# A pair loop rewritten as a software pipeline with a fixed issue order on three engines

## The chip, the cores and the metric

One core of a Trainium2 chip. The time is the device time of one execution in microseconds (us). All kernels named here gave the right result. Each measured kernel was run four times or more, beside runs of the kernel before on the same chip. All comparisons use runs in the fast state. A ratio below is the mean time of one kernel's fast runs over the mean of the other's fast runs of the same rounds, so it is not quite the ratio of the medians quoted beside it. The profile's engines are PE (TensorE), PEld (its weight load), DVE (VectorE), ACT (ScalarE), POOL (GpSimd).

## The reference, cut to what matters

```python
# layer 0: every node i against every node j of 3327 (padded to 26 blocks of 128), 64 features
h = relu(layernorm(x))
adj_att = sigmoid(left[:, None] + right[None, :] + b_att[0]) * adj
x_local = logmap(h[:, None, :], h[None, :, :], c)        # a scalar function of i.j times two vectors
support_t = einsum('ij,ijd->id', adj_att, x_local)
x = x + proj(expmap(h, support_t, c), c)                 # the "post step", per node
# layer 1: weights 2^-(k - pos) from a running count of each row's edges
rank = cumsum(adj != 0, axis=1)                          # [...]
x = x + (mask * where(pos > 0, 0.5 ** (k - pos), 0)) @ (relu(layernorm(x)) @ weight) + bias
```

Layer 0 and the running count of layer 1 go through the adjacency matrix together, so that it is read once.

## The kernel before

The columns are cut into four strips of 8, 8, 6 and 4 blocks. In a strip the kernel goes through the rows from the last block to the first, one block of 128 rows per round (two in strip 3, whose rows of the tile are half as long). The order on each engine is left to the scheduler. `T`, `V`, `A` are TensorE, VectorE, ScalarE.

```python
STRIPS = [(0, 8), (8, 8), (16, 6), (22, 4)]
for b0, nb in STRIPS:
    # [...] loads of the strip's iu, iz
    for b in range(nb):                                    # the row `left`, laid over all partitions
        T.transpose(pl[:, b * P : (b + 1) * P], left[:, b0 + b : b0 + b + 1].to_broadcast([P, P]), ident)
    A.copy(left_b[:, :F], pl[:, :F])
    for f0, f1 in hv:                                      # a constant under the count
        T.matmul(pc[:, f0:f1], row1, rowc[:, : f1 - f0], start=True, stop=True, skip_group_check=True)
    for hi in range(NB, 0, -per):                          # one round
        # [...] ad: the adjacency tile by DMA
        V.tensor_scalar(mask[:, :span], ad[:, :span], 0.0, None, op0=ALU.not_equal)        # "mask"
        for j in js:
            # [...] per half: two matmuls into pc, with ca on the last mask and cb on this one ("count")
            if j % (2 if b0 == 0 else 4):
                A.activation(kept, pc[:, :F], AF.Relu)                                      # "the read"
            else:
                V.tensor_scalar(kept, pc[:, :F], 0.0, None, op0=ALU.max)                    # the same on VectorE
        for j in js:
            A.activation(part(sg, j), left_b[:, :F], AF.Tanh, bias=right[:, j : j + 1], scale=0.5)
        V.scalar_tensor_tensor(sg[:, :span], sg[:, :span], 1.0, ad[:, :span], op0=ALU.add, op1=ALU.mult)
        # [...] products of iu and iz with ju and jz into pq
        A.activation(s[:, :span], pq[:, :span], AF.Gelu, scale=-WG / QS)
        A.activation(s[:, :span], s[:, :span], AF.Gelu, scale=WH)
        V.scalar_tensor_tensor(s[:, :span], s[:, :span], WD, sg[:, :span], op0=ALU.add, op1=ALU.mult)
        for j in js:
            # [...] per half: T.matmul(po, hw, s)                                           # "total"
            next(steps, None)                              # one part of the last strip's post step
    # [...] po to SBUF, transposes, two ScalarE copies, the next post step is made ready
```

A post step is some 60 operations on VectorE with three Square and one tanh on ScalarE between them; among them are three reciprocal roots, each of 12 tiny operations of 128x8, nearly every one of which needs the last.

## Time and profile before

The time is 461.0 us (459.1 to 463.9, four runs). The stages below are read from the starts of VectorE's last multiply of a round (`s`): a strip goes from its first `s` to its last, a seam from there to the next strip's first.

| stage before | us |
|---|---|
| start to first `s` | 52.5 |
| strip 0, 1, 2, 3 | 87.0, 92.1, 73.3, 47.7 |
| the three seams | 12.5, 10.45, 9.7 |
| last `s` to the end | 73.9 |

Of the page's list of groups (line, operation, tiles, count, then busy us, mean ns, then us of idle time just before them and what ended it), these two matter later, and of the table of stretches strip 3 (the columns after the stretch are its length, busy us of PE, PEld, DVE, ACT, POOL with counts, the granted TensorE clock, DMA share and GB/s):

```profile
L852 DVE SCALAR_TENSOR_TENSOR s<-s,sg 128x1024 f32<-128x1024 f32 (+1 forms) x91 | 104.8, 1152 | 3.7 <-ACT s L851 3.6
L855 PE MATMUL po<-s,hw 128*65 128x512 f32 (+1 forms) x364 | 165.3, 576 | 11.5 <-DVE s L852 11.1
```
```profile
337.00:385.00 48.00, 40.44 (x126) 13.23 (x125) 46.88 (x98) 46.23 (x68) 1.00 (x1) 0.99 0.34 99
```

VectorE waits 3.7 us for the Gelus in the whole kernel, TensorE 11.5 us for `s`. In strip 3 VectorE is busy 46.9 of 48 us. There is almost nothing to win inside a strip, and less in the seams than their 32.6 us suggest: VectorE is busy in 28.1 of them, with masks, multiplies, reads and the copy of `po`. From the first `s` to the last it stands idle for 12.2 of 332.8 us.

### The profile page before, as it was taken

How to read it: one execution, taken by the hardware profiler on the slowest of the kernel's cores; microseconds unless marked ns; L12 is line 12 of the kernel's file. 1: busy time of each engine (PE TensorE's matmuls, PEld its weight loads, DVE VectorE, ACT ScalarE, POOL GpSimd, SP SyncE). 2: the span in 40 equal slices, each digit the busy share in tenths (PEclk: the TensorE clock that was granted, in tenths of full speed). 3: DMA queues.
4: the chain of work that ended last, by engine and by line, in shares of the span. 5: the costliest groups of instructions: out<-in, count | busy, mean ns of one | idle time of the engine just before them, and what ended most of it. 6: DMA issues, size and time to landing. Idle time of an engine off the chain costs nothing.

```text
span 459.1 us, 4660 instructions
## 1 busy us (share of the span) xinstructions
PE 378.4 (82%) x1484; PEld 153.4 (33%) x1484; DVE 407.1 (89%) x774; ACT 369.2 (80%) x423; POOL 13.3 (3%) x30
## 2 busy tenths in 40 slices
PE   0266699999989799999997999889778897699293
PEld 0035233333323233333333444434322332244152
DVE  3895689999988999999998999999999998999821
ACT  1445989999894999999995999999599995888310
POOL 6000000000000000001000000020000000000000
PEclk9997699999999999999999999999999998899877
DMA  7103354545541444444442444344533420000003
GB/s 201 62 1 72 105 168 143 141 151 163 167 135 46 133 143 140 137 137 137 137 127 75 136 137 140 106 128 125 168 93 111 121 89 1 1 1 1 0 0 82
DMA packets 22840, 47.77 MB, mean 104 GB/s; under 512 B 8652, under 2 KB 9082, under 8 KB 22808
## 3 DMA queue, kind: packets, MB, share of 16 engines
q1 hardware_dynamic: 20522, 46.47, 34.7%
q10 hardware_dynamic: 2062, 0.87, 0.9%
q0 software_dynamic: 224, 0.07, 0.3%
q8 instruction: 13, 0.21, 0.2%
q14 instruction: 19, 0.16, 0.1%
HBM read 45.22 MB, written 0.85 MB: 100 GB/s over the span
## 4 chain that ended last, share of the span: by engine, by line

## 5 line engine op out<-in xcount | busy, mean ns | idle before, releaser
L855 PE MATMUL po<-s,hw 128*65 128x512 f32 (+1 forms) x364 | 165.3, 576 | 11.5 <-DVE s L852 11.1
L842 DVE SCALAR_TENSOR_TENSOR sg<-sg,ad 128x1024 f32<-128x1024 f32 (+1 forms) x91 | 103.5, 1141 | 7.5 <-ACT sg L841 7.3
L852 DVE SCALAR_TENSOR_TENSOR s<-s,sg 128x1024 f32<-128x1024 f32 (+1 forms) x91 | 104.8, 1152 | 3.7 <-ACT s L851 3.6
L841 ACT ACTIVATE sg<-left_b,right 128x1024 f32<-128x1024 f32 (+2 forms) x104 | 102.7, 1001 | 0.1
L851 ACT ACTIVATE s<-s 128x1024 f32<-128x1024 f32 (+1 forms) x91 | 91.4, 1006 | 0.1
L850 ACT ACTIVATE s<-pq 128x1024 f32<-128x1024 f32 (+1 forms) x91 | 87.7, 969 | 2.6 <-PE pq L848 2.6
L829 PE MATMUL pc<-mask,ca 128*128 128x512 bf16 (+1 forms) x175 | 65.7, 375 | 17.3 <-DVE behind_hi L836 7.2
L855 PEld LDWEIGHTS po<-s,hw 128*65 128x65 f32 x364 | 45.2, 138 | 98.9 <-issue 52.7
L847 PE MATMUL pq<-iu,ju 71*128 71x512 f16 (+1 forms) x182 | 67.8, 374 | 11.6 <-ACT s L850 11.6
L830 PE MATMUL pc<-mask,cb 128*128 128x512 bf16 (+1 forms) x182 | 66.7, 376 | 5.3 <-DVE mask L824 5.1
L848 PE MATMUL pq<-iz,jz 128*128 128x512 f16 (+1 forms) x182 | 66.6, 371 | 0.0
L824 DVE TENSOR_SCALAR mask<-ad 128x1024 bf16<-128x1024 f32 (+1 forms) x91 | 59.3, 654 | 3.4 <-PE pc L829 1.8
L894 PE MATMUL pw<-wt,s 128*128 128x512 bf16 (+1 forms) x182 | 41.0, 390 | 12.9 <-DVE s L782 9.2
L834 ACT ACTIVATE behind_hi<-pc 128x1024 uint8<-128x1024 f32 (+2 forms) x37 | 31.8, 860 | 24.3 <-PE pc L830 24.1
L830 PEld LDWEIGHTS <-cb 128*128 128x128 bf16 x182 | 17.9, 99 | 57.8 <-issue 46.6
L834 ACT ACTIVATE behind_lo<-pc 128x1024 uint8<-128x1024 f32 (+2 forms) x33 | 28.2, 853 | 7.1 <-PE pc L830 6.4
L894 PEld LDWEIGHTS <-s 128*128 128x128 f16 x182 | 18.7, 103 | 35.0 <-DVE s L782 9.6
L848 PEld LDWEIGHTS <-jz 128*128 128x128 f16 x182 | 18.1, 99 | 31.5 <-issue 15.3
L829 PEld LDWEIGHTS <-ca 128*128 128x128 bf16 x175 | 17.5, 100 | 30.8 <-issue 19.5
L847 PEld LDWEIGHTS <-ju 71*128 71x128 f16 x182 | 18.1, 100 | 21.4 <-issue 4.8
L836 DVE TENSOR_SCALAR behind_lo<-pc 128x1024 uint8<-128x1024 f32 (+2 forms) x19 | 19.9, 1050 | 1.1 <-PE pc L830 1.1
L771 POOL TENSOR_TENSOR x_sb<-x_sb,bias_b 128x512 f32<-128x512 f32 (+2 forms) x4 | 6.3, 1577 | 418.4 <-DVE w L769 418.4
(209 smaller groups left out, 290.0 us busy)
## 6 DMA issues: line engine op xcount, KB each, us to landing
ad<-in_adj_t SPq DMA_DIRECT2D x65, 512.0 KB, 3.7
ad<-in_adj_t SPq DMA_DIRECT2D x26, 384.0 KB, 3.3
out<-o SPq DMA_DIRECT2D x6, 128.0 KB, 2.0
x_sb<-in_x SPq DMA_DIRECT2D x1, 416.0 KB
x_sb<-in_x ACTq DMA_DIRECT2D x1, 416.0 KB, 6.9
iz<-jz ACTq DMA_DIRECT2D x2, 128.0 KB
iz<-jz SPq DMA_DIRECT2D x2, 128.0 KB, 2.4
iz<-jz SPq DMA_DIRECT2D x2, 96.0 KB
```

The costliest lines, as they stand in the source:

```text
L829: T.matmul(pc[:, f0:f1], ca, before[:, f0:f1], start=False, stop=True, skip_group_check=True)
L830: T.matmul(pc[:, f0:f1], cb, now[:, f0:f1], start=False, stop=True, skip_group_check=True)
L834: A.activation(kept, pc[:, :F], AF.Relu)
L841: A.activation(part(sg, j), left_b[:, :F], AF.Tanh, bias=right[:, j : j + 1], scale=0.5)
L842: V.scalar_tensor_tensor(sg[:, :span], sg[:, :span], 1.0, ad[:, :span], op0=ALU.add, op1=ALU.mult)
L847: T.matmul(part(pq, j, f0, f1), ju[:KB, j, :], iuf[:, f0:f1], start=True, stop=False)
L848: T.matmul(part(pq, j, f0, f1), jz[:, j, :], izf[:, f0:f1], start=False, stop=True)
L850: A.activation(s[:, :span], pq[:, :span], AF.Gelu, scale=-WG / QS)
L851: A.activation(s[:, :span], s[:, :span], AF.Gelu, scale=WH)
L852: V.scalar_tensor_tensor(s[:, :span], s[:, :span], WD, sg[:, :span], op0=ALU.add, op1=ALU.mult)
L855: T.matmul(po[: D + 1, f0:f1], hw[:, j, :], part(s, j, f0, f1), start=j == NB - 1, stop=j == 0)
L894: T.matmul(pw[n], s2[:, j].rearrange("p c d -> p (c d)"), wt[:, f0:f1].bitcast(BF16), start=j == 0, stop=j == NB - 1)
```

## The change

Its intent is to keep the engines running across the seams, by writing the four strips as one list of rounds, and to fix what each engine issues in which order. In round n TensorE totals n-1, multiplies for n+1 and counts for n+2. A strip's `left` row comes by a broadcast DMA from a DRAM copy, and not by transposes. The diff, cut to its core:

```diff
+ON_ACT = ((1, 2), (3, 4), (3, 4), (3, 4))          # share of the reads on ScalarE: nearly as before, 73 reads for 70
-    for f0, f1 in hv:
-        T.matmul(pc[:, f0:f1], row1, rowc[:, : f1 - f0], start=True, stop=True, skip_group_check=True)
+        # [...] strip_in(k), strips 1 to 3:
+            nc.sync.dma_start(S.left[:, : S.F], bass.AP(tensor=left_d.tensor, offset=left_d.offset + S.i0,
+                                                         ap=[[0, P], [1, S.F]]))
+    tc_order = tc.manual_schedule(engines={mybir.EngineType.DVE, mybir.EngineType.Activation, mybir.EngineType.PE})
+    with tc_order:
+        products(0)
+        sigmoids(0)
+        for n in range(R):
+            # [...] m = n + 2; `new` is a strip's first round, `second` its second (strips 1 to 3)
+            if second:
+                steps = strip_out2(k - 1)                # transposes, ScalarE copies, post step
+            elif n:
+                total(n - 1)
+            A.activation(s[:, :w], pq[:, :w], AF.Gelu, scale=-WG / QS)
+            A.activation(s[:, :w], s[:, :w], AF.Gelu, scale=WH)
+            sg_inst[n] = V.scalar_tensor_tensor(sg[:, :w], sg[:, :w], 1.0, ad_of.pop(n)[:, :w], [...])
+            if new:
+                strip_out(k - 1)                         # po to SBUF
+            read()                                       # a VectorE read, if one is due
+            if m < R:
+                edges(m)                                 # mask
+            if two:
+                count(m, js(m)[0])                       # with its ScalarE read, if one is due
+            if n + 1 < R:
+                products(n + 1)
+                sigmoids(n + 1)                          # tanh
+            for _ in js(n):
+                next(steps, None)                        # one part of the post step, as a block
+            # [...] a strip's last round runs the rest of the steps
+            read()
+            if m < R:
+                count(m, js(m)[-1])                      # with its ScalarE read, if one is due
+            V.scalar_tensor_tensor(s[:, :w], s[:, :w], WD, sg[:, :w], op0=ALU.add, op1=ALU.mult)
+            if second:
+                total(n - 1)
```

So on ScalarE a round is: Gelu, Gelu, tanh, and a read of the count of round n+2, which stands ahead of the Gelus of round n+1.

Not shown in the cut, but part of the change: five buffers for `ad` instead of four and two for `left_b` instead of one, the copy of `po` in a buffer of `sg` and its transposes in one of `po` (before: `s` and `pq`), and the range check of the inputs, spread over the first rounds and finished in layer 1.

## The prediction

> **What bounds the kernel now.** The kernel does layer-0 attention over all pairs in four strips of columns (8, 8, 6 and 4 blocks of 128). Each round of a strip makes, per 128x1024 tile: a mask (VectorE), a running count into the PSUM tile `pc` (TensorE) which is then read to bytes (ScalarE or VectorE, "the read"), a tanh, a product `pq` (TensorE), two Gelus (ScalarE), two VectorE multiplies (first `sg`, last `s`), and the total into `po` (TensorE). A strip's result is finished by a post step of some 60 small VectorE instructions that runs during the next strip. Layer 1 follows, from 392 us on. I read the page first (busy shares), then the table of stretches with the cuts at the first and last `s` of each strip, then the timelines of VectorE and ScalarE for start-to-start distances, then the built instruction orders of both kernels.
>
> ```profile
> PE 378.4 (82%) x1484; PEld 153.4 (33%) x1484; DVE 407.1 (89%) x774; ACT 369.2 (80%) x423; POOL 13.3 (3%) x30
> ```
> VectorE is the busiest. The stretches show where:
>
> ```profile
> 52.00:139.00 87.00, 84.10 (x275) 30.05 (x274) 82.35 (x83) 82.07 (x86) 0.00 (x0) 0.97 0.52 154
> 139.00:152.00 13.00, 11.41 (x52) 4.78 (x51) 11.10 (x22) 6.95 (x10) 0.00 (x0) 1.00 0.04 10
> 152.00:244.00 92.00, 85.94 (x283) 29.89 (x283) 90.94 (x152) 90.64 (x98) 2.19 (x1) 1.00 0.49 142
> 244.00:254.00 10.00, 8.33 (x45) 4.07 (x44) 7.95 (x14) 5.38 (x9) 0.00 (x0) 1.00 0.08 29
> 254.00:328.00 74.00, 66.46 (x283) 29.75 (x282) 73.60 (x157) 71.45 (x98) 2.40 (x1) 1.00 0.49 138
> ```
> After the length come PE, weight load, VectorE, ScalarE. In strips 1 and 2 VectorE is busy 91 of 92 and 74 of 74 us; in strip 0 all three engines are above 94%. The seams (139 to 152, 244 to 254, also 328 to 337) lose time.
>
> The prices, from start to start on VectorE in strip 0:
>
> ```profile
> 84.32 0.69 DVE L824 TENSOR_SCALAR mask<-ad 128x1024 bf16<-128x1024 f32 x1
> 84.92 1.22 DVE L842 SCALAR_TENSOR_TENSOR sg<-sg,ad 128x1024 f32<-128x1024 f32 x1
> 86.06 0.69 DVE L824 TENSOR_SCALAR mask<-ad 128x1024 bf16<-128x1024 f32 x1
> 86.66 1.22 DVE L852 SCALAR_TENSOR_TENSOR s<-s,sg 128x1024 f32<-128x1024 f32 x1
> 87.80 1.22 DVE L836 TENSOR_SCALAR behind_hi<-pc 128x1024 uint8<-128x1024 f32 x1
> ```
> A mask costs 0.60, each multiply and a VectorE read 1.135. Strip 0 reads every second count on VectorE: 0.60 + 2.5 x 1.135 = 3.44 us a round. Its `s` tiles run from 52.46 to 139.44, 25 intervals of 3.48: VectorE's issue rate. Strip 1 has a quarter of the reads: 25 x 3.15 = 78.9, plus the post step, 16 tiles of 512 columns at 0.60 and some 47 tiny ones at 0.08: 13.4. Sum 92.3; measured (151.90 to 244.03) 92.1. Strip 2 (254.48 to 327.77) took 73.3 against 60.8 + 13.4. So inside the strips VectorE has no slack, and only the seams can be won.
>
> A tiny operation costs only 0.08 because the scheduler puts it ahead of a big one:
>
> ```profile
> 225.73 0.16 DVE L511 TENSOR_TENSOR rs_t<-rs_t,rs_g 128x8 f32<-128x8 f32 x1
> 225.81 0.69 DVE L824 TENSOR_SCALAR mask<-ad 128x1024 bf16<-128x1024 f32 x1
> 226.41 0.16 DVE L512 SCALAR_TENSOR_TENSOR rn<-rs_t,rn 128x8 f32<-128x8 f32 x1
> 226.49 1.22 DVE L852 SCALAR_TENSOR_TENSOR s<-s,sg 128x1024 f32<-128x1024 f32 x1
> ```
> One after the other, each needing the last, they stand 0.20 apart, as in layer 1:
>
> ```profile
> 433.35 0.17 DVE L507 TENSOR_SCALAR rn<-rs_t 128x4 int32<-128x4 int32 x1
> 433.56 0.16 DVE L510 TENSOR_TENSOR rs_t<-rn 128x4 f32<-128x4 f32 x1
> 433.75 0.16 DVE L511 TENSOR_TENSOR rs_t<-rs_t,rs_g 128x4 f32<-128x4 f32 x1
> ```
> And the hops between engines:
>
> ```profile
> 127.45 1.06 ACT L851 ACTIVATE s<-s 128x1024 f32<-128x1024 f32 x1
> ...
> 128.55 1.23 DVE L852 SCALAR_TENSOR_TENSOR s<-s,sg 128x1024 f32<-128x1024 f32 x1 [0.64 <-ACT s L851]
> ...
> 137.29 1.03 ACT L850 ACTIVATE s<-pq 128x1024 f32<-128x1024 f32 x1
> ...
> 138.35 1.06 ACT L851 ACTIVATE s<-s 128x1024 f32<-128x1024 f32 x1
> ...
> 151.90 1.21 DVE L852 SCALAR_TENSOR_TENSOR s<-s,sg 128x1024 f32<-128x1024 f32 x1
> ...
> 153.27 1.88 PE L855 MATMUL po<-s,hw 128*65 128x512 f32 x4
> ```
> ScalarE to VectorE 0.04; the second Gelu starts 1.06 after the first when nothing stands between; VectorE to the total's first matmul 0.10 to 0.16. A total is 4 matmul passes of 0.43 (1.71), products and count 4 of 0.215 each (0.86). On ScalarE, start to start, tanh costs 1.04, a read 0.90.
>
> **What the skill says.** "Perfetto Trace Analysis", Sequencer Loop: an engine's instructions go into a queue and wait there for their semaphores; so in a fixed order a late operand holds up all behind it. The trace agrees: VectorE stood 0.64 us before `s` above. The same page, Identifying Performance Opportunities, says to improve the most-contended engine by its occupancy, here VectorE. "VectorE: DVE Perf Modes", The DRAIN you can't avoid, measures that a semaphore between chained copies "costs nothing extra". This trace differs for tiny tiles: 0.20 with a dependence, 0.08 without. The measurement decides. "ScalarE: Activation LUTs", What ACT_TABLE_LOAD costs, gives about 280 ns + 0.833 ns per element with a pointer bias, 186 without, and 93 of overlap; for 1024 columns 1.13 and 1.04, here 1.165 (tanh) and 1.03 (Gelu).
>
> **The change part by part.** 1. Removed: the constant matmuls into `pc`, and for strips 1 to 3 the transposes of `left` and their ScalarE copy (1.01 us each, replaced by a DMA issued about three rounds ahead, hidden). All lie at seams.
>
> 2. Fixed order. Per round n: TensorE total(n-1), products(n+1), count(n+2); ScalarE Gelu, Gelu (n), tanh(n+1), read(n+2); VectorE sg(n), read, mask(n+2), one post step, s(n). No big tile's work changes, so VectorE's floor of 3.44 stays. But the order closes a loop: s(n-1) ends; 0.10 to total(n-1), 1.71; products 0.86; count 3 x 0.215 + 0.38 = 1.03; 0.05; read(n+2) on ScalarE 0.90; only then Gelu, Gelu (n+1) 1.06 + 1.07; 0.04; s(n+1) 1.22. Sum 8.04 for two rounds, 4.02 each, wherever the read falls to ScalarE: every second round of strip 0, and rounds two apart in the others. Strip 0: 25 x (4.02 - 3.48) = +13.5.
>
> 3. Post steps in one block per round. The built order shows each reciprocal root as 12 chained tiny operations with nothing between: about 2.3 us instead of 1.0, three times, and the step of 14 behind the tanh 2.5 instead of 1.1. Adding up the steps with 0.20 for a dependent and 0.08 for a free one gives 22.7 instead of 13.4. Strip 1: VectorE alone 78.9 + 22.7 = 101.6, +9.5; taking the loop in the 21 light rounds (84.4) and 2.87 + 2.6 in the four heavy ones (21.9), 106.3, +14. I take +13. Strip 2: the loop at 768 columns is about 3.14 a round; 21 x 3.14 + 19.3 = 85, against VectorE alone 83.5; I take +11. Strip 3 takes two steps a round: 12 x 3.17 + 20.4 (six-block steps) = 58.4 against 47.7 (337.51 to 385.24); some may lie in waits, +10.
>
> 4. Seams. Before, from last `s` to first `s`: 12.5, 10.4, 9.7, sum 32.6. After, the next strip's rounds are already running: VectorE waits for total(n-1) (about 2.2), copies `po` (1.13), mask and s, about 5.5, and the round behind it (transposes, two ScalarE copies) about 1.2 longer: 19 in all. Gain -13.5.
>
> 5. The end: total, copy, transposes straight behind the last `s`, 4.9 instead of 6.7: -1.5 with rounding. The range check's few tiny operations move into layer 1: +1.
>
> Sum: 13.5 + 13 + 11 + 10 - 13.5 - 1.5 + 1 = +33.5; 460.6 + 33.5 = 494.
>
> **The rivals.** (a) The pipeline works as meant: engines even out, tiny operations hide, only the seams change: 460.6 - 15 = 446. For it: the seams' idle time is real. Against it: VectorE is in order, and the chained tiny operations stand in one block. (b) Only VectorE counts, the loop has slack I don't see (the hops are from few instances): 0 + 9.5 + 10 + 10 - 13.5 - 0.5 = +15.5, 476. (c) Loop and heavy rounds add up fully, and the seams give less because the second total of a strip is delayed behind the transposes: about 505. (d) TensorE's clock: slices 4 and 5 of the page show 7 and 6 tenths granted; a loop through TensorE feels that more than a kernel bound by VectorE: +3 to +5.
>
> **Range and chances.** Between (b) and (c), with a little below (b): 472 to 508. Rival (a) is all that gives a gain, and I give it 0.07; a balance within 2% 0.08; slower 0.85.
>
> **What would show it.** Right: in strip 0 the `s` tiles start about 4.0 apart by pairs, ScalarE idles about 1 us before each read, released by the count's matmul, and VectorE waits on ScalarE before `s`; in strips 1 and 2 the rounds with a reciprocal root take over 5 us and VectorE's busy share falls; seams shrink to 5 to 7 us. Wrong: strip 0 still at 3.5 a round (loop not there), or tiny operations 0.08 apart in a block, or seams as long as before. If the reads stop being waited for, the time falls toward 476.

## More of the kernel before

`pc` and `po` have one buffer each in PSUM (two banks each), `pq` has two.

## The result, and the profile after

The changed kernel took 513.24 us (512.39 to 516.8, four runs), the kernel before 461.03 in the same rounds: 1.114 times as long (95% interval 1.106 to 1.122). The direction was as predicted; the size was not, and 513 lies above the range. All outputs are right.

```profile
PE 385.7 (75%) x1442; PEld 153.0 (30%) x1460; DVE 418.8 (81%) x772; ACT 381.7 (74%) x423; POOL 10.6 (2%) x28
```
```profile
L906 PE MATMUL po<-s,hw 128*65 128x512 f32 (+1 forms) x364 | 172.2, 597 | 66.0 <-DVE s L982 65.8
L982 DVE SCALAR_TENSOR_TENSOR s<-s,sg 128x1024 f32<-128x1024 f32 (+1 forms) x91 | 106.0, 1165 | 29.4 <-ACT s L959 29.3
...
L875 ACT ACTIVATE behind_lo<-pc 128x1024 uint8<-128x1024 f32 (+2 forms) x36 | 30.3, 841 | 32.0 <-PE pc L868 31.8
L875 ACT ACTIVATE behind_hi<-pc 128x1024 uint8<-128x1024 f32 (+2 forms) x37 | 31.3, 845 | 26.5 <-PE pc L868 25.6
```

No engine works much longer than before (VectorE 418.8 for 407.1 us), and every share fell. The groups say who waits for whom, and it is a ring: TensorE's total waits 66.0 us for `s` (11.5 before), `s` 29.4 us for the second Gelu (3.7 before), and ScalarE's reads 58.5 us for the count (before, 31.4 us). The stretches of the four strips after:

```profile
51.00:154.00 103.00, 92.92 (x292) 31.57 (x298) 87.93 (x94) 88.89 (x89) 0.00 (x0) 0.97 0.44 129
...
158.00:269.00 111.00, 90.53 (x304) 31.80 (x308) 101.20 (x165) 96.92 (x102) 1.27 (x1) 1.00 0.39 114
273.00:363.00 90.00, 70.80 (x305) 31.38 (x306) 83.03 (x164) 76.41 (x102) 1.27 (x1) 1.00 0.40 114
368.00:443.00 75.00, 55.73 (x143) 18.24 (x144) 56.21 (x125) 49.98 (x72) 1.00 (x1) 0.82 0.18 55
```

In strip 0 VectorE was busy 82 of 87 us, now 88 of 103; in strip 3, 47 of 48, now 56 of 75, with a granted clock of 0.82 instead of 0.99. Set against each other stage by stage (profiled executions of 459.1 and 515.1 us):

| stage | before | after | difference | predicted |
|---|---|---|---|---|
| strip 0 | 87.0 | 102.6 | +15.6 | +13.5 |
| strip 1 | 92.1 | 110.1 | +18.0 | +13 |
| strip 2 | 73.3 | 89.7 | +16.4 | +11 |
| strip 3 | 47.7 | 74.6 | +26.9 | +10 |
| three seams | 32.6 | 14.9 | -17.7 | -13.5 |
| start, end of the loop, layer 1 | 126.4 | 123.3 | -3.1 | -0.5 |

The differences add up to +56.1, the spans differ by 56.0. Two cautions: the profiled execution of the change was the slowest of its four (516.8 us, the others 512.4 to 514.0), so some 3 or 4 us may be that execution's own; and a stage can gain by handing work to its neighbour. VectorE was busy in 12.0 of the 14.9 us of the seams after, for 28.1 of 32.6 before, so most of the seams' -17.7 is work that now lies in the strips.

The loop itself, as the timeline shows it in strip 0 (start and duration in us; in brackets the idle time before, and what ended it):

```profile
61.94 1.02 ACT L875 ACTIVATE behind_hi<-pc 128x1024 uint8<-128x1024 f32 x1 [1.25 <-PE pc L868]
...
65.00 1.22 DVE L982 SCALAR_TENSOR_TENSOR s<-s,sg 128x1024 f32<-128x1024 f32 x1 [1.23 <-ACT s L959]
...
66.14 1.22 DVE L961 SCALAR_TENSOR_TENSOR sg<-sg,ad 128x1024 f32<-128x1024 f32 x1
...
66.28 1.93 PE L906 MATMUL po<-s,hw 128*65 128x512 f32 x4 [0.80 <-DVE s L982]
...
67.28 1.22 DVE L882 TENSOR_SCALAR behind_hi<-pc 128x1024 uint8<-128x1024 f32 x1
...
68.41 0.68 DVE L856 TENSOR_SCALAR mask<-ad 128x1024 bf16<-128x1024 f32 x1
...
69.15 0.81 PE L868 MATMUL pc<-mask,cb 128*128 128x512 bf16 x2
...
69.99 1.02 ACT L875 ACTIVATE behind_hi<-pc 128x1024 uint8<-128x1024 f32 x1 [0.95 <-PE pc L868]
```

From one ScalarE read to the next but one round's is 69.99 - 61.94 = 8.05 us; the working of the prediction had 8.04. It splits into 3.06 us from the read through the two Gelus to `s`, and 4.99 us from `s` back to the read. The prediction followed that second part through TensorE: total at 66.28, then products and count, 69.15. But VectorE closes it at the same length: behind `s` come `sg`, its own read and the mask, and the mask ends at 69.09, just before the count that needs it starts at 69.15. From here on nobody can say from the trace alone which of the two holds the loop.

The post steps in strip 1, in the same view:

```profile
212.03 1.23 DVE L982 SCALAR_TENSOR_TENSOR s<-s,sg 128x1024 f32<-128x1024 f32 x1 [0.80 <-ACT s L959]
...
215.91 0.17 DVE L508 TENSOR_TENSOR rs_t<-rn 128x8 f32<-128x8 f32 x1
216.12 0.17 DVE L509 TENSOR_TENSOR rs_t<-rs_t,rs_g 128x8 f32<-128x8 f32 x1
...
217.26 1.22 DVE L982 SCALAR_TENSOR_TENSOR s<-s,sg 128x1024 f32<-128x1024 f32 x1
```

The tiny operations stand 0.20 apart, and this round took 217.26 - 212.03 = 5.23 us. The four heavy rounds of strip 1 (three with a reciprocal root, one with the 14 operations behind the tanh) took 5.54, 5.48, 5.23 and 5.17, together 21.4 where 21.9 was predicted; the other 21 took (110.05 - 21.42) / 21 = 4.22 instead of 4.02. Among these are two of 5.07 and 5.63 us, in which a VectorE read and a part of the post step fall together.

For strip 3, the view of waits on VectorE (what waited, for whom, then us in all, times, longest), and below it TensorE's costliest wait there:

```profile
DVE sg L961 <- ACT sg L889: 7.5, 5, 2.7
DVE t L782 <- ACT dt L779: 2.3, 1, 2.3
DVE t L765 <- ACT dt L762: 2.3, 1, 2.3
DVE u L732 <- ACT dt L725: 2.0, 1, 2.0
```
```profile
PE po L906 <- DVE s L982: 15.9, 7, 3.8
```

With a tanh of the post step (1.6 us) these are 15.7 us of VectorE standing still, against 1.1 us idle in all before. The prediction has no term for either kind.

### The profile page after: what moved, and what is told of

It reads as the page before. It is cut to its first block, busy times and chain, and to the rows that moved or that the text cites. A ratio compares the mean times of both kernels' runs of the same rounds, so it can differ in the third digit from the quotient of the medians.

```text
span 515.1 us, 4572 instructions
## 1 busy us (share of the span) xinstructions
PE 385.7 (75%) x1442; PEld 153.0 (30%) x1460; DVE 418.8 (81%) x772; ACT 381.7 (74%) x423; POOL 10.6 (2%) x28
## 4 chain that ended last, share of the span: by engine, by line
## 5 line engine op out<-in xcount | busy, mean ns | idle before, releaser
L906 PE MATMUL po<-s,hw 128*65 128x512 f32 (+1 forms) x364 | 172.2, 597 | 66.0 <-DVE s L982 65.8
L982 DVE SCALAR_TENSOR_TENSOR s<-s,sg 128x1024 f32<-128x1024 f32 (+1 forms) x91 | 106.0, 1165 | 29.4 <-ACT s L959 29.3
L889 ACT ACTIVATE sg<-left_b,right 128x1024 f32<-128x1024 f32 (+2 forms) x104 | 100.0, 974 | 0.0
L868 PE MATMUL pc<-mask,cb 128*128 128x512 bf16 (+1 forms) x178 | 65.2, 376 | 21.2 <-DVE mask L856 20.5
L896 PE MATMUL pq<-iu,ju 71*128 71x512 f16 (+1 forms) x182 | 70.0, 384 | 0.0
L897 PE MATMUL pq<-iz,jz 128*128 128x512 f16 (+1 forms) x182 | 68.2, 382 | 0.0
L867 PE MATMUL pc<-mask,ca 128*128 128x512 bf16 (+1 forms) x165 | 61.5, 373 | 4.6 <-ACT behind_hi L875 2.3
L875 ACT ACTIVATE behind_lo<-pc 128x1024 uint8<-128x1024 f32 (+2 forms) x36 | 30.3, 841 | 32.0 <-PE pc L868 31.8
L896 PEld LDWEIGHTS <-ju 71*128 71x128 f16 x182 | 18.5, 102 | 34.3 <-issue 21.9
L1002 ACT ACTIVATE wt<-behind_lo 128x3328 uint16<-128x3328 uint8 x6 | 17.4, 2963 | 0.0
L882 DVE TENSOR_SCALAR behind_lo<-pc 128x1024 uint8<-128x1024 f32 (+2 forms) x16 | 17.1, 1067 | 0.0
```

What stands on the lines that cost most here:

```text
L867: T.matmul(S.pc[:, f0:f1], ca, S.before[:, f0:f1], start=False, stop=True, skip_group_check=True)
L868: T.matmul(S.pc[:, f0:f1], cb, now[:, f0:f1], start=S.first, stop=True, skip_group_check=True)
L875: A.activation(kept, S.pc[:, : S.F], AF.Relu)
L889: A.activation(part(n, sg, j), S.left[:, : S.F], AF.Tanh, bias=right[:, j : j + 1], scale=0.5)
L896: T.matmul(part(n, pq, j, f0, f1), ju[:KB, j, :], S.iu[:, f0:f1], start=True, stop=False)
L897: T.matmul(part(n, pq, j, f0, f1), jz[:, j, :], S.iz[:, f0:f1], start=False, stop=True)
```

## The experiments

Theory at the start: the loop through ScalarE's read costs strip 0 and the light rounds, blocks of chained tiny operations cost the heavy rounds, and in strip 3 the read in the middle of a round holds up the tanhs. Rivals: the loop is held by VectorE's order or by the one `pc` buffer and not by TensorE; and removing any one wait brings out another. The strip lengths in this table (us, first to last `s`) come from each run's profile; medians and ratios to the kernel before from all fast runs.

| kernel | median | ratio (95%) | strip 0 | strip 1 | strip 2 | strip 3 |
|---|---|---|---|---|---|---|
| before | 461.0 | 1 | 87.0 | 92.1 | 73.3 | 47.7 |
| after | 513.2 | 1.114 (1.106, 1.122) | 102.6 | 110.1 | 89.7 | 74.6 |
| late_read | 502.5 | 1.093 (1.088, 1.097) | 92.4 | 105.1 | 89.6 | 74.9 |
| spread | 497.6 | 1.082 (1.078, 1.086) | 102.6 | 107.3 | 86.2 | 62.1 |
| mid_read | 513.8 | 1.119 (1.114, 1.124) | 101.6 | 110.5 | 91.2 | 69.3 |
| lag2 | 507.5 | 1.101 (1.096, 1.106) | 101.3 | 108.4 | 89.4 | 67.4 |
| mask_first | 516.7 | 1.123 (1.118, 1.127) | 104.4 | 110.3 | 90.4 | 72.8 |
| mask_lag2 | 512.7 | 1.115 (1.109, 1.121) | 103.4 | 110.1 | 89.0 | 68.5 |
| all3 | 477.7 | 1.036 (1.031, 1.040) | 92.1 | 102.7 | 83.4 | 59.2 |
| all3_lag2 | 474.8 | 1.029 (1.025, 1.033) | 88.7 | 102.4 | 83.2 | 56.9 |
| before_row | 449.7 | 0.974 (0.971, 0.978) | 87.5 | 89.1 | 73.8 | 42.9 |
| auto | 444.8 | 0.967 (0.963, 0.970) | 87.7 | 95.2 | 77.3 | 44.6 |
| only_act | 496.1 | 1.076 (1.071, 1.082) | 101.4 | 107.0 | 90.2 | 60.6 |
| only_dve | 478.5 | 1.038 (1.031, 1.044) | 89.5 | 100.2 | 82.7 | 66.6 |
| only_pe | 459.6 | 0.998 (0.996, 1.001) | 95.5 | 97.1 | 79.1 | 47.5 |

The medians of the kernel before in the four groups of rounds lay between 460.3 and 461.1, so medians of different groups may be set side by side.

### The read behind the Gelus (late_read), or between them (between_read)

```diff
-            A.activation(kept, S.pc[:, : S.F], AF.Relu)
+            act_reads.append((kept, S.pc[:, : S.F]))
             A.activation(s[:, :w], pq[:, :w], AF.Gelu, scale=-WG / QS)
+            # between_read: act_read() here
             A.activation(s[:, :w], s[:, :w], AF.Gelu, scale=WH)
+            # late_read: act_read() here
```

> The ScalarE read that ends a round is emitted behind the two Gelus of the next round instead of ahead of them; nothing else changes. Theory (the loop of 8.04 us per two rounds goes through that read, and the post steps add on top of it): without it strip 0 falls from 4.10 to about 3.5 us a round (102.6 to 89 us from first to last s tile), strip 1 from 110 to about 102 (VectorE with its block of chained tiny operations, worked out as 101.6), strip 2 from 89.7 to about 84, strip 3 stays near 72 to 75; the time 513 to about 484. Rival (only the post step's chained operations and the clock cost time, the read merely waits where there is slack): strip 0 stays at 4.0, the time within 2% of 513.

> The same read emitted between the first and the second Gelu of the next round. Theory: the loop loses one Gelu of 1.06 us, 6.98 instead of 8.04 per two rounds, so 3.49 a round, just above VectorE's 3.44; strip 0 about 88 us, the time within 1% of the kernel with the read behind both Gelus. Rival (it is not the length of the loop that matters but that ScalarE waits for the count at all): a gain of about half or less.

late_read took 502.5 us where 484 was expected. Strip 0 fell from 102.6 to 92.4, with steady rounds of 3.63 instead of 4.03, and strip 1 from 110.1 to 105.1. The read no longer waits; it starts as soon as ScalarE is free:

```profile
69.10 1.01 ACT L884 ACTIVATE behind_hi<-pc 128x1024 uint8<-128x1024 f32 x1
```

Strips 2 and 3 did not move; 84 us had been expected for strip 2, and why it stayed is open. between_read took 494.7 us, 1.073 times before (1.067 to 1.078), from three fast runs; its profiled run was slow, so its strips are not used. It had been expected within 1% of late_read and is 1.5% faster; why is not shown. Moving the read won back 11 to 18 of the 52 us. Strip 0 did not come all the way to 3.5: in late_read VectorE now waits a little for the tanh, which has the read ahead of it.

### Post steps handed out in small pieces (spread)

```diff
-        rsqrt(pool, rn, t0, nb)                      # 12 tiny operations in a block
+        yield from rsqrt_g(pool, rn, t0, nb)         # a yield after each dependent one
         A.activation(dt, u, AF.Square)
-        yield
+        yield HOLD                                   # two slots free before its result is used
```

A slot is behind `sg`, behind a VectorE read, ahead of `s` and behind `s`.

> The post step cut into single dependent operations, one in each gap between wide VectorE instructions, with two gaps left free behind each result that comes from ScalarE; the reads stay as in the change. Theory: strip 0 unchanged at 102 us; strip 1 falls from 110 to the loop's 4.02 x 25 = 100.5 to 102, strip 2 from 89.7 to about 80; strip 3 loses the 8.2 us in which VectorE waits for ScalarE inside the post step and the block stalls, 74.6 to about 60; the time 513 to about 481. Rival (the loop through the read is all, the tiny operations sit in its slack): strips 1 and 2 within 2 us of before, the time 505 or more.

497.6 us: 15.6 us better than the change, of which strip 3 alone gave 12.5 in the profiles (74.6 to 62.1). In strips 1 and 2 the gain was 2.8 and 3.5 us, less than half of what was expected. In strip 1 the heavy rounds exceed the others by 21.4 - 4 x 4.22 = 4.5 us in all, so no more than that was to be had while the loop held the others; I had not done this sum, and this half of the expectation missed. In strip 3 the 8.2 us of waits for the Squares and the post step's tanh are gone from the trace, `sg` still waits 5.0 us for the tanh, and the clock is 0.97; how much the smaller pieces and how much the free slots did, one run cannot tell.

### The middle read of strip 3 behind the tanhs (mid_read)

```diff
             if two:
-                count(m, js(m)[0])                   # its ScalarE read at once, ahead of both tanhs
+                count(m, js(m)[0])
             sigmoids(n + 1)
+            if two:
+                act_read()
```

> Only in strip 3 (two blocks a round): the ScalarE read in the middle of a round is emitted behind the two tanh instead of ahead of them. Theory: the tanh no longer waits for count, which waits for the total, which waits for s; the 7.5 us in which VectorE waits in strip 3 for the tanh before sg go away; strip 3 from 74.6 to 67 or 68, the time 513 to about 506, strips 0 to 2 unchanged. Rival (strip 3 is slow because of TensorE's clock of 0.82 and the post step's waits): strip 3 within 2 us of 74.6.

In the profile strip 3 fell by 5.3 us, a little less than expected, but the median did not move (513.8 for 513.2). The profiled run of the change was the slowest of its four (516.8), that of mid_read the fastest of its own (511.5), so part of the 5.3 us may be the choice of runs. This one is inconclusive in time. Its trace is clearer: in strip 3 `sg` no longer waits for the tanh at all (7.5 us before), so the read's place made that wait; but the first Square of the post step is now waited for 5.1 us instead of 2.0, which takes part of the gain back.

### What closes the loop (lag2, mask_first, mask_lag2)

```diff
-                total(n - 1)                         # lag2, mask_lag2: one round later
+                total(n - 2)
-            read()                                   # mask_first, mask_lag2: VectorE's read after the mask
             edges(m)
+            read()
```

> The total into po lags by two rounds instead of one (total(n-2) in round n; at a seam both are done at once); the reads stay ahead of the Gelus as in the change. Theory: the loop is broken at another of its links, since count and read no longer stand behind a total that waits for the newest s; strip 0 falls from 4.10 to 3.5 or 3.6 a round as with the late read (the read's place was never the fault by itself), strips 1 and 2 as with the late read (about 105 and 88 us), the time about 500. Rival (the place of the read on ScalarE is what costs, whatever stands behind it): strip 0 stays at 4.0 a round, the time within 1% of 513.

> VectorE's mask for the round after next is emitted ahead of its read instead of behind it; total one round late and ScalarE's read ahead of the Gelus as in the change. Theory after the two-rounds-late total left strip 0 at 4.05: there are two loops of the same length, both through ScalarE's read and the two Gelus; one comes back over s, total, products and count (8.04), the other over s, sg, VectorE's read and mask to count (about 8.1). This run breaks only the second: strip 0 stays at 4.0 to 4.1 a round, the time within 1% of 513. Rival (the mask loop alone binds): strip 0 at 3.6 or less.

> Mask ahead of the read, and the total two rounds late. Theory of the two loops: now both are broken though ScalarE's read still stands ahead of the Gelus; the second loop is shorter by one VectorE instruction of 1.135, 6.98; strip 0 at 3.5 to 3.65 a round, 88 to 92 us; the time about 490 to 497. Rival (the read's place on ScalarE costs in itself): strip 0 at 4.0, the time above 503.

If TensorE's total held the loop, lag2 would cut strip 0. It stayed at 4.05 us a round, as its rival said. The count now waited for the mask:

```profile
107.45 0.38 PE L868 MATMUL pc<-mask,cb 128*128 128x512 bf16 x1 [0.22 <-DVE mask L856]
```

If the mask were the only other way, mask_lag2 would have brought 3.5. It brought 8.27 for two rounds and 512.7 us, so its rival was right; mask_first gave the same 8.27, near the 4.0 to 4.1 a round that its theory said. The reason is in the trace of mask_lag2: VectorE's read of the single `pc` buffer now ends later, and the next count starts only behind it:

```profile
99.81 0.38 PE L867 MATMUL pc<-mask,ca 128*128 128x512 bf16 x1 [1.20 <-DVE behind_lo L882]
```

So between `s` and the next ScalarE read lie three ways back, through the total, the mask and the VectorE read, the last two over the same engine, and all about 5 us long (4.99 us in the change, 5.00 in lag2, 5.26 in mask_lag2). Of the cuts that were tried only the one in the part that they share, the read ahead of the Gelus, paid in strip 0: late_read. lag2's gain of 5.8 us in the median lies in strip 3 (-7.2 in the profiles), not in the loop.

### The mended pipeline (all3, all3_lag2)

all3 is late_read with spread and the middle read behind the tanhs; all3_lag2 adds lag2.

> Late read, single post operations in the gaps and strip 3's middle read behind the tanh together. Theory (the causes are separate and share the strips): strip 0 3.70 as with the late read alone, strip 1 about 97, strip 2 about 79, strip 3 about 55; the time about 513 - 10 - 13 - 11 - 20 = 459, within 1% of the kernel before. Rival (they hide behind one another or a further wait takes their place): 475 or more.

> The same with the total two rounds late as well. Theory: TensorE then never waits for the newest s, so strip 0 comes to VectorE's 3.44 to 3.5 a round, strip 1 to 93 to 95, strip 2 to 75 to 77, strip 3 to 50 to 52; the time about 450, below the kernel before thanks to the shorter seams. Rival (the fixed order keeps some 0.2 us of wait in each round): about as long as without the lag.

They took 477.7 and 474.8 us and remain 3 to 4% slower than the kernel before; the rivals' numbers held, not the theory's. all3_lag2's strip 0 is nearly mended (88.7 against 87.0), strips 1 to 3 are not (102.4, 83.2 and 56.9 against 92.1, 73.3 and 47.7). In strip 1, VectorE's `sg` waited in 8 times for the tanh, which now stands behind the read, 4.6 us in all3 and 4.3 in all3_lag2. Each order that I wrote down by hand moved a wait somewhere else. all3 is still 33 us slower than the same rounds without a fixed order (auto, below), so about half of what the order costs is not traced to a cause by these runs.

### The row by DMA without the rest (before_row)

```diff
-        for b in range(nb):
-            T.transpose(pl[:, b * P : (b + 1) * P], left[:, b0 + b : b0 + b + 1].to_broadcast([P, P]), ident)
-        A.copy(left_b[:, :F], pl[:, :F])
+        if b0 == 0:
+            # [...] the two lines above
+        else:
+            nc.sync.dma_start(left_b[:, :F], bass.AP(tensor=left_d.tensor, offset=left_d.offset + i0, ap=[[0, P], [1, F]]))
```

> The kernel before with one part of the change alone: the left row of strips 1 to 3 by a broadcast from DRAM in place of transposes and a ScalarE copy; the order stays the scheduler's. Theory (this part lies at the seams only and is worth little): 0 to 3 us faster, 458 to 461, ratio 0.993 to 1.0. Rival (the broadcast of 512 KB comes late and holds the first tanh of a strip): slower by 3 us or more, with a wait for the DMA before the first tanh of strips 1 to 3.

449.7 us, 2.6% faster than before; 0 to 3 us had been expected. The seams fell from 32.6 to 26.6 us, and strips 1 and 3 by 3.0 and 4.8; the end, from the last `s`, grew by 3.4, since part of a post step moved there. The edit also gives `left_b` a second buffer, and a copy of `left` to DRAM at the start, both cut here. How much of the gain is the missing transposes, how much the second buffer and how much the scheduler's other order of everything, these runs do not separate.

### The changed kernel without its fixed order (auto), and with it on one engine

```diff
-    tc_order = tc.manual_schedule(engines={mybir.EngineType.DVE, mybir.EngineType.Activation, mybir.EngineType.PE})
-    with tc_order:
+    if True:                                         # auto; only_dve, only_act, only_pe: one engine in the set
```

> The changed kernel without its fixed order: the same instructions emitted in the same sequence of rounds, but the scheduler orders them as in the kernel before. Theory (the fixed order is all that costs, the other parts are gains): 445 to 452, with strips 0 to 3 near 87, 92, 74, 46 us. Rival (emitting by rounds or the earlier loads and buffers cost by themselves): 465 or more.

> Only VectorE keeps the fixed order; ScalarE and TensorE are left to the scheduler (which alone gave 445). Theory (the loop needs ScalarE's read ahead of the Gelus, the block of chained post operations needs only VectorE): strip 0 at 3.5 to 3.6 a round (88 to 91), strip 1 101 to 104, strip 2 83 to 86, strip 3 55 to 62; the time 470 to 480. Rival (the losses need all three orders together): below 455.

> Only ScalarE keeps the fixed order. Theory: the part that all loops share is on ScalarE (read, Gelu, Gelu), but the ways back over VectorE and TensorE may be shortened by the scheduler, so strip 0 at 3.6 to 4.0 a round, and no block of post operations, so strips 1 and 2 within 5 us of the scheduler's 95 and 77; the time 450 to 465. Rival (ScalarE's order alone makes the loop): strip 0 at 4.0 or more, the time above 465.

> Only TensorE keeps the fixed order. Theory: neither ScalarE's read nor the block is fixed, so little is lost: strip 0 at 3.5 to 3.65, the time 445 to 453. Rival (a total that stands ahead of products and count is what starves ScalarE): strip 0 at 3.8 or more, the time above 460.

auto took 444.8 us: the same rounds, buffers, split of the reads and the DMA row, only left to the scheduler. It is 3.3% faster than the kernel before, and the fixed order alone costs 513.2 - 444.8 = 68 us. In strips 0 and 1 all three engines are close to full:

```profile
50.00:138.00 88.00, 86.36 (x281) 30.89 (x282) 85.60 (x87) 84.73 (x88) 0.00 (x0) 0.96 0.54 162
140.00:235.00 95.00, 92.31 (x317) 32.87 (x316) 94.71 (x161) 94.39 (x105) 3.31 (x1) 1.00 0.46 135
```

VectorE is busy 85.6 of 88 us and 94.7 of 95; the seams are 2.0, 2.9 and 4.1 us. Its strips 1 and 2 are 3 to 4 us longer than in the kernel before and the end 4.8, since much of the work of the seams (9.0 us for 32.6), and more of the last post step, now lies there. What is really saved shows from the first `s` to the last: VectorE stands idle for 2.8 us there, for 12.2 in the kernel before and 53.5 in the change.

Of the single engines, ScalarE's order costs 51 us over auto, VectorE's 34, TensorE's 15. They are not to be added (100 for 68), since a wait that two orders cause is paid once. ScalarE's order alone gives two rounds of strip 0 in 4.54 + 3.41 = 7.95 us, with both other engines free to move; I had expected 450 to 465 us for it and the rival was right. For TensorE's order alone I had expected 445 to 453 us and 3.5 to 3.65 us a round in strip 0; it took 459.6 and 3.82, in rounds of 5.20 and 2.28 by turns, so that missed too, and its cause was not looked for further. VectorE's order alone leaves strip 0 near the bound (89.5) and brings strip 1 to 100.2 and strip 2 to 82.7, where the prediction had worked out 101.6 and 83.5 for VectorE with chained blocks and no loop. In its strip 3 the waits for the Squares are there too (3.0, 2.9 and 1.3 us), the one of `sg` for the tanh is not.

## Why the prediction was right or wrong

**Step 1, removed matmuls and transposes at seams.** Right that they lie at the seams, too small in worth: before_row gained 11 us, with nothing but the row and its second buffer changed.

**Step 2, the loop.** Right in its length, 8.05 for 8.04, in who pays (the ScalarE read waits about 1 us for the count) and in its cost: +15.6 for +13.5 in strip 0, the rest being the second and third intervals of 5.76 and 4.46 us. TensorE's clock was halved until 57.6 us, in the second of them; in mid_read, whose strip 0 has the same order, it was full from 54.9 us on, and the two took 4.79 and 4.46. So about 1 us is the clock, as rival (d) said, and the rest is not. What it had wrong is that the loop is *one* way back. It has three of nearly the same length, and the part to blame is the shared one: the read ahead of the Gelus. (The 1.13 and 1.04 us that the prediction works out from the page on ScalarE are estimates; the 1.165 and 1.03 beside them are the trace's.)

**Step 3, strips 1 and 2.** The heavy rounds were right to 0.5 us in sum (21.4 for 21.9). The term "I take +13" chose a value between two workings, and the higher of them, 106.3 us or +14, was still short: the 21 other rounds took 4.22 instead of 4.02 each, 4.2 us more. 106.3 - 0.5 + 4.2 = 110.0 is what was measured. About 1.6 us of it is the first two rounds of the strip (4.60 and 5.07 us), which step 4 had booked under the seams. Strip 2, +16.4 for +11, went the same way: loop and blocks add up, and no value between the two is to be taken.

**Step 3, strip 3: this is the step that failed.** "12 x 3.17 + 20.4 = 58.4 ... some may lie in waits, +10". It measured +26.9. VectorE's busy time rose by 9.3 us (46.9 to 56.2), so the work that the step counted came out. What it left out was waiting, in two kinds. One: with two post parts in each round, a part waits inside the round for a Square or a tanh on ScalarE that was issued in the part before, 2.3 + 2.3 + 2.0 + 1.6 = 8.2 us; only_dve shows these with VectorE's order alone. Two: the middle read stands ahead of both tanhs on ScalarE and waits for the count, which stands behind the total, which waits for `s`; so `sg` waits for the tanh, 7.5 us. Both are shown by a run that takes them away: in spread, which breaks up the blocks and keeps two slots free before a ScalarE result is used, the first kind is gone and strip 3 is 12.5 us shorter; in mid_read the second kind is gone. I looked at VectorE's order for what it *does*, and not at what each piece *needs*.

The third part of strip 3 is the clock, 0.82. The Trainium skill, "TensorE: Matmul & The Clock Gate", HAM oscillation — how this bites in real kernels, warns of idle gaps on TensorE above some 3.4 us. This agrees in part: TensorE's longest wait in strip 3 was 3.8 us, in strips 1 and 2 it was 1.9 and 2.1 at a clock of 1.00. Across the variants, the longest wait in strip 3 and the clock go together, though not strictly: 3.8 and 0.82 (after), 3.7 and 0.86 (only_dve), 4.0 and 0.88 (mid_read), 3.6 and 0.90 (only_act), 1.8 and 0.97 (spread), 0.8 and 1.00 (auto). But the clock also fell where no wait was that long, to 0.96 in strip 2 of lag2 (longest 2.4 us) and to 0.94 in that of only_act (2.6), so the traces bear out no limit. On this reading the low clock is a result of the waits that lengthens them in turn, but that is argued from these pairs. How many us it adds is open; no run changed the clock alone.

**Step 4, seams.** Right in kind: 5.0, 4.9 and 5.0 us. The sum was -17.7 for -13.5; with 1.6 us given back for the first rounds of each strip, an estimate from strip 1, it is -12.9. What the prediction read as lost time was mostly work, though: its own line of the first seam has VectorE busy in 11.1 of 13 us, and such work does not go away when the seam gets short. "Only the seams can be won" was the wrong reading of those lines.

**Step 5, the end.** -1.8 for the copy behind the last `s` (predicted -1.5, though its own 4.9 for 6.7 gives -1.8), +0.4 for the rest (predicted +1). The start was 1.6 us shorter, for which there was no step.

**The range.** Rival (c), 505, was the nearest, since the parts do add up; it was held to be the edge of the range when it should have been its middle. Rival (a), 446, is near what the same pieces give when nothing fixes their order (444.8), in part by luck: it had -15 from the seams alone, where auto has -23.6 there, +4.6 in the strips, +4.8 at the end and -2.1 at the start. It was the order that spoilt it, as was argued against (a) there.

## What to carry to other kernels

Before you fix the order on engines that issue in order, walk round the loop through all of them, and ask of every instruction that waits for another engine what stands behind it: here a read that nobody needed soon stood ahead of two Gelus that everybody needed, and moving it won back 11 to 18 us. When one return way is broken and the time stays, look for a second of the same length, and cut the part they share. Before you count a gap as time to be won, look whether the busiest engine works in it. And try the parts of a change alone: the row by DMA alone won 11 us, all of the change but the order 16, and the order lost 68; the version to keep is auto, at 444.8 us.

## What the Trainium skill lacked or had wrong

- "VectorE: DVE Perf Modes", The DRAIN you can't avoid: the semaphore that "costs nothing extra" was measured on chained copies. For tiny operations of 128x8, a dependent one starts 0.20 us after the last one, while one slipped in between big ones costs 0.08. No page that was looked at gives a figure for the dependent one. Left to the scheduler strip 1 took 95.2 us, with VectorE's order fixed and the tiny ones in blocks 100.2, though these two differ in more than the tiny ones.
- "Perfetto Trace Analysis", Identifying Performance Opportunities: it puts consistent bubbles down to too little SBUF or PSUM for the next tile, as a possibility. Here the bubble of about 1.1 us ahead of `s` in every second round of strip 0 has its cause in the issue order: with the same tiles and buffers and no fixed order, strip 0 takes 87.7 us instead of 102.6.
- No page I read tells that a loop across engines can be closed by several ways of nearly the same length, so that undoing one shows nothing: here 8.05 us for two rounds in the change, 8.27 with the other order of mask and read, with or without the later total, and 7.95 with ScalarE's order alone.
